# The table of token slots in a routed mixture-of-experts kernel: rows made list by list with scalars by partition, 64 places by 286 half blocks

## The chip, the cores and the metric

The kernel runs on one core of a Trainium2 chip, one launch. The metric is the device time of one execution in microseconds (us). The kernel before took 1169.23 us, the median of 3 runs (1165.0 to 1175.48).

Engines are named as in the profile: PE is TensorE (PEld its weight loads), DVE is VectorE, ACT is ScalarE, POOL is GpSimd, SP is SyncE. Every engine works through its own instructions in order.

## The reference

The kernel computes one layer on 8 sequences of 512 tokens with 512 features:

```
xn = layernorm(x)
s  = attention(xn)      # 16 heads of 32, chunks of 128, a decayed linear attention, gate, group norm, @ Wo
g  = silu(moe(xn))      # 16 experts, each token to its best 4, plus a shared expert
x  = x + s * g
```

and the part that matters here:

```
router_probs = softmax(flat @ gate_w.T)
routing_weights, selected_experts = top_k(router_probs, 4)
routing_weights = routing_weights / routing_weights.sum(-1)
mixed = sum over e of comb[:, e] * (silu(flat @ Wg[e]) * (flat @ Wu[e]) @ Wd[e])
```

There are 4096 tokens with 4 choices each: 16,384 pairs of a token and an expert.

## The kernel before

The work goes in four stages.

1. All sequences are normed, transposed and routed, and the shared expert is computed. Sequence 0 of the attention runs along.
2. The pairs are sorted by expert into blocks of 128 rows. `sort()` (lines 372 to 466) finds for each pair its position in the sorted order; an expert's rows begin at a multiple of 128, so there are at most `NB` = 143 blocks. `table()` (lines 469 to 559) turns this around: `slot[p, b]` is to be the token that stands in row p of block b. Sequence 1 of the attention runs along (`sequence(1, ...)`, line 1043).
3. Each block gathers its tokens' rows by `slot` (L1071, an indirect DMA on POOL), is multiplied with its expert's weights (L1112, L1133) and written back.
4. The other six sequences of the attention run, and each token gathers its four expert rows and adds them up.

The table is made from 128 lists (`TOPK * NT` = 4 choices by 32 tiles of tokens). A list holds one pair per partition, with its place in its block (`sp[:, 0]`, 0 to 127) and its block (`sp[:, 1]`, 0 to 142). For each list there are two matrices in f16 with a row per partition: `place` has the token's number at the pair's place and zeros elsewhere, `block` has a one at the pair's block. `place.T @ block` puts the tokens where they belong, and the sum over all lists is the table.

`make()` (L510, L513, L516) makes these rows on DVE, 8 lists in one instruction, by comparing a count with the positions, which are broadcast along the rows. For that the lists stand interleaved by four (`QUAD`): the elements of one list's row are four elements apart. L513 multiplies in the token's number for half the lists; ACT does it for the other half (`number()`, L524, one instruction per list, with a scalar by partition). PE multiplies list after list into one bank (L545, 128 matmuls of 143 columns), 16 lists in a group (`GROUP`); after each group DVE adds the bank to `acc` (L553, L555). L558 turns `acc` into `slot`. The scratch lies in the place of the last four experts' weights (`wexp`), so the profile calls these tiles `wexp`; the weights are loaded there when the table is done with each half (L537 on SP's queue, L1049 on ACT's).

What sets the order: `table()` is a generator. The attention's `value()` and `product()` call `between[0]()` after each of their matmuls on 128 contraction rows (lines 590 and 634), and each call runs the generator to its next `yield`. `sequence(1, ...)` makes 32 such calls; line 1044 runs what is left. `on_pe()` pins PE to the order in which the code is written; on the other engines a scheduler places the instructions when the program is built. The lines that the working uses beside these: L643 to L647 rotate a head group's queries and keys, L708 and L710 make its states, L720 masks its scores, L714 scales its queries, L742 and L746 make its output, L764 is a reciprocal in the group norm, L773 and L778 apply it, L785 projects. L236 and L1007 are two earlier instructions on DVE (the norm of x; a scaling of `wo`).

Of the kernel before, what the change touches and what calls it, by code (L numbers as in the profile page):

```python
# [10 lines left out]
F32 = mybir.dt.float32  # L11
# [4 lines left out]
AF = mybir.ActivationFunctionType  # L16
ALU = mybir.AluOpType
AX = mybir.AxisListType

P = 128  # L20
B, N, D = 8, 512, 512
# [4 lines left out]
NT = B * NC  # L26
KC = D // P
E, F, TOPK = 16, 128, 4
# [7 lines left out]
NB = (B * N * TOPK + E * (P - 1)) // P  # L36
WE = KC * 2 * F + D
# [3 lines left out]


SURE = B * N * TOPK // P + E // 2
QUAD = 4
LATE = 4
GROUP = 16


SWAP = [(i + HD // 2) % HD for i in range(HD)]
# [46 lines left out]
def tile_block(ctx: ExitStack, tc: tile.TileContext, a: dict, out: bass.AP):  # L96
    nc = tc.nc
# [7 lines left out]
    def bank(tag, name):  # L105
        return pp.tile([P, 512], F32, tag=tag, name=name, bufs={"a": 4, "k": 1, "m": 1, "d": 2}[tag])
# [11 lines left out]
    def load(pool, name, shape, dt=F32):  # L118
        t = pool.tile(shape, dt, tag=name, name=name, bufs=1)
        flat = t if len(shape) == 2 else t.rearrange(  # L120
            "p a b -> p (a b)" if len(shape) == 3 else "p a b c -> p (a b c)")
        nc.sync.dma_start(flat, a[name])
        return t
# [30 lines left out]
    ident = load(const, "ident", [P, P])  # L154
# [7 lines left out]
    token = load(const, "token", [P, NT])  # L162
# [27 lines left out]
    posi = p1.tile([P, TOPK, NT], I32, tag="posi", name="posi")  # L190

    sp = const.tile([P, 2, TOPK * NT], F16, tag="slot", name="sp")
# [11 lines left out]
    @contextmanager  # L204
    def on_pe():

        with tc.issue_after(last_pe[-1]) if last_pe else nullcontext():
            yield
        traced = nc.cur_bb.bb.instructions
        last_pe.append(next(  # L210
            i for i in reversed(traced) if i.engine == mybir.EngineType.PE))

    def behind(engine):

        last = next(
            (i for i in reversed(nc.cur_bb.bb.instructions) if i.engine == engine), None)
        return tc.issue_after(last) if last else nullcontext()
# [154 lines left out]
    def sort():  # L372
# [22 lines left out]
        at = p1.tile([P, E, NT], F32, tag="at", name="at")  # L395
# [40 lines left out]
        bl = p1.tile([P, 2, TOPK, NT], I32, tag="bl", name="bl")  # L436
        for r in range(TOPK):
            nc.gpsimd.tensor_tensor(oa[:, r], oh[:, r], at, ALU.mult)
            with behind(DVE):
                nc.vector.tensor_reduce(  # L440
                    pos[:, r], oa[:, r].rearrange("p e t -> p t e"), axis=AX.X, op=ALU.add)
            with behind(DVE):
                nc.vector.tensor_copy(posi[:, r], pos[:, r])
            with behind(DVE):
                nc.vector.tensor_scalar(bl[:, 0, r], posi[:, r], P - 1, None, ALU.bitwise_and)
            with behind(DVE):
                nc.vector.tensor_scalar(bl[:, 1, r], posi[:, r], 7, None, ALU.logical_shift_right)
            with behind(DVE):
                nc.vector.tensor_copy(
                    sp.rearrange("p w (r t) -> p w r t", t=NT)[:, :, r], bl[:, :, r])  # L450
            yield
# [17 lines left out]
    def table(room):  # L469

        half = room.bitcast(F16)
        free = [0]
        quads = GROUP // QUAD


        def part(*shape):
            n = int(np.prod(shape))
            free[0] += n  # L480
            flat = half[:, free[0] - n : free[0]]
            return flat.rearrange("p (q j) -> p q j", j=QUAD) if len(shape) == 2 else (
                flat.rearrange("p (u q j) -> p u q j", u=quads, j=QUAD))

        homes = [(part(quads, P, QUAD), part(quads, NB, QUAD))]
        free[0] = WE * LATE
        homes.append((part(quads, P, QUAD), part(quads, NB, QUAD)))
        count = part(NB, QUAD)
        half_token = half[:, free[0] : free[0] + NT]
        free[0] += NT  # L490
        nc.scalar.copy(half_token, token)
        acc = room[:, free[0] // 2 :][:, :NB]
        nc.gpsimd.iota(
            count, [[1, NB], [0, QUAD]], base=0, channel_multiplier=0,
            allow_small_or_imprecise_dtypes=True)

        def rows(of, n):
            return of.rearrange("p (u j) -> p u j", j=QUAD).unsqueeze(2).to_broadcast(
                [P, of.shape[-1] // QUAD, n, QUAD])

        def make(i):
            place, block = homes[i // GROUP % 2]
            for u in range(0, quads, 2):
                us = slice(u, u + 2)
                lists = slice(i + u * QUAD, i + (u + 2) * QUAD)

                def counts(n):
                    return count[:, :n].unsqueeze(1).to_broadcast([P, 2, n, QUAD])

                nc.vector.tensor_tensor(  # L510
                    place[:, us], counts(P), rows(sp[:, 0, lists], P), ALU.is_equal)
                if u == 0:
                    nc.vector.tensor_tensor(  # L513
                        place[:, us], place[:, us], rows(half_token[:, lists.start % NT :][
                            :, : 2 * QUAD], P), ALU.mult)
                nc.vector.tensor_tensor(  # L516
                    block[:, us], counts(NB), rows(sp[:, 1, lists], NB), ALU.is_equal)

        def number(i, some):
            place = homes[i // GROUP % 2][0]  # L520
            for j in range(max(some[0], GROUP // 2), some[1]):
                row = place[:, j // QUAD, :, j % QUAD]
                t = (i + j) % NT
                nc.scalar.activation(row, row, AF.Copy, scale=token[:, t : t + 1])  # L524

        yield
        make(0)
        for j in range(0, GROUP, QUAD):
            number(0, (j, j + QUAD))
            yield  # L530
        for i in range(0, TOPK * NT, GROUP):
            more = i + GROUP < TOPK * NT
            if more:
                make(i + GROUP)
            else:
                for e in range(E - LATE, E - LATE // 2):
                    nc.sync.dma_start(wexp[:, e, :], a["experts"][:, e, :])  # L537
            if i < TOPK * NT // 2:
                yield
            place, block = homes[i // GROUP % 2]  # L540
            pn = bank("a", f"pn_{i}")
            for some in ((0, 5), (5, 10), (10, GROUP)):
                with on_pe():
                    for j in range(*some):
                        nc.tensor.matmul(  # L545
                            pn[:, :NB], lhsT=place[:, j // QUAD, :, j % QUAD],
                            rhs=block[:, j // QUAD, :, j % QUAD], start=(j == 0),
                            stop=(j == GROUP - 1))
                if more:
                    number(i + GROUP, some)  # L550
                if some[1] == GROUP:
                    if i:
                        nc.vector.tensor_tensor(acc, acc, pn[:, :NB], ALU.add)  # L553
                    else:
                        nc.vector.tensor_copy(acc, pn[:, :NB])  # L555
                yield
        t = const.tile([P, NB], I32, tag="slot", name="slot")
        nc.vector.tensor_scalar(t, acc, float(B * N // 2), None, ALU.add)  # L558
        slots.append(t)


# [17 lines left out]
    kept, carry, blocked = [], [], []  # L579
# [391 lines left out]
    def first():  # L971
# [22 lines left out]
        next(sorting)  # L994

    sorting = sort()
    norm(0)
    turn(0)
# [33 lines left out]
    wexp = exps.tile([P, EA - 1, WE], F32, tag="wexp", name="wexp")  # L1032
# [5 lines left out]
    for i in range(SURE, NB):  # L1038
        nc.sync.dma_start(y_d[i * P : (i + 1) * P, :], none)
    filling = table(wflat[:, (E - LATE) * WE :])  # L1040
    next(filling)
    between[0] = lambda: next(filling, None)
# [16 lines left out]
    more = att.tile([P, 2 * NC * D], U16, tag="v", name="more", bufs=2)  # L1059
    homes = [blkp.tile([P, ROW], U16, tag=f"xg{j}", name=f"xg{j}") for j in range(4)]  # L1060
# [136 lines left out]
    place = comb.tile([P, TOPK, NT], I32, tag="place", name="place")  # L1197
# [166 lines left out]
```

## Time and profile before

| what | us |
|---|---|
| median of 3 runs | 1169.23 |
| the profiled execution's own time | 1169.4 |
| its span, first to last instruction | 1167.6 |
| PE busy in the span | 1134.0 (97%) |
| DVE, ACT, POOL busy | 705.6, 460.2, 452.2 |
| first instruction of the table on DVE (L510) | at 227.61 |
| `slot` written (L558) | at 301.66 |
| first gather by it (L1071) | at 302.81 |
| first expert matmul (L1112) | at 318.61 |
| mean granted clock of TensorE | 0.996 |

A line of a group reads: line, engine, operation, output<-inputs, output shape<-input shape, count; then the busy time and the mean length of one in ns; then the idle time of the engine before these instructions and what ended it. A line of the order in time reads: start, time until the last end, engine, line, operation, tiles, shapes, count, and in brackets an idle time before it. An instruction's length runs into the next one's: on DVE the next starts some 0.08 us before the end of the one before. So the price of an instruction in a row of its kind is the time from start to start. A line of busy times by stretch gives the stretch, its length, then for PE, PEld, DVE, ACT and POOL the busy us (and the instructions), the granted clock, the busy share of the DMA engines and their GB/s.

### The profile page before, as it was taken

The page shows a single profiled execution, that of the slowest core. Times are in us where ns is not written, and L with a number is a line of the kernel's source. Part 1 is how long each engine was busy: PE and PEld are TensorE (multiplying, and loading weights), DVE is VectorE, ACT ScalarE, POOL GpSimd, SP SyncE. Part 2 cuts the span into 40 slices and gives each one's busy share as a digit, 9 for nine tenths or more (in the row PEclk, how much of TensorE's full clock was granted, in tenths as well). Part 3 has the DMA queues.
Part 4 walks back from the last instruction along what each step waited for, and adds up shares of the span by engine and source line. Part 5 has one row for each costly group of instructions (what it writes and reads, how often), then busy time and mean ns, then how long its engine had stood idle before and what let it go on. Part 6 is the DMA issues. An engine that isn't in the chain of part 4 may idle for free. (4 is left out here: it accounts for less than half of the span.)

```text
span 1167.6 us, 21692 instructions
## 1 busy us (share of the span) xinstructions
PE 1134.0 (97%) x7780; PEld 694.6 (59%) x7780; DVE 705.6 (60%) x1496; ACT 460.2 (39%) x1042; POOL 452.2 (39%) x432
## 2 busy tenths in 40 slices
PE   7999999989999999999999999999999999999997
PEld 3445554455577677777777775555554645545553
DVE  6358735996134344444444443968879598697784
ACT  3323324254364444444444442352252532523541
POOL 3213103200223333333333331782886858858211
PEclk9999999998999999999999999999999999999999
DMA  9975521290769989999999996951846637535012
GB/s 341 330 251 186 179 106 46 101 361 2 232 153 227 219 228 219 229 233 218 230 223 231 230 226 159 359 148 64 277 128 181 215 100 255 154 119 153 28 38 72
DMA packets 163787, 217.45 MB, mean 186 GB/s; under 512 B 89824, under 2 KB 99168, under 8 KB 161760
## 3 DMA queue, kind: packets, MB, share of 16 engines
q1 hardware_dynamic: 142272, 144.14, 41.9%
q0 software_dynamic: 21120, 70.34, 22.3%
q8 instruction: 65, 1.06, 0.4%
q10 hardware_dynamic: 288, 1.57, 0.4%
q14 instruction: 42, 0.34, 0.1%
HBM read 125.73 MB, written 72.43 MB: 170 GB/s over the span
## 5 line engine op out<-in xcount | busy, mean ns | idle before, releaser
L1112 PE MATMUL pgu<-wexp,xt 128*128 x1088 | 257.9, 380 | 2.7 <-ACT xt L1093 2.2
L1112 PEld LDWEIGHTS pgu<-wexp,xt 128*128 128x128 f32 x1088 | 205.8, 190 | 90.4 <-issue 29.5
L1071 POOL DMA_INDIRECT xg<-xn_d,slot x79 | 74.9, 948 | 243.0 <-DVE y L1142 156.4
L1095 ACT COPY xt<-pl 128x512 uint16<-128x512 uint16 x136 | 104.3, 767 | 142.9 <-DMA pl<-xg 75.9
L1117 DVE TENSOR_TENSOR slb<-slb,pgu 128x128 f32<-128x128 f32 x136 | 39.1, 288 | 196.6 <-ACT slb L1116 196.5
L1215 POOL DMA_INDIRECT yg<-y_d,place x128 | 142.4, 1112 | 31.4 <-issue 18.4
L1133 PE MATMUL py<-wexp,hT 128*128 x272 | 139.2, 594 | 0.0
L587 PE MATMUL pv<-wv,xT 128*128 128x512 f32 x256 | 122.2, 614 | 3.8 <-DMA xT<-xT_d 2.8
L631 PE MATMUL pk<-xT,wk 128*128 128x512 f32 x256 | 118.3, 603 | 0.0
L631 PE MATMUL pq<-xT,wq 128*128 128x512 f32 x256 | 115.9, 593 | 0.3 <-PEq L1177 0.3
L785 PE MATMUL pw<-wo,on 128*128 128x512 f32 x224 | 100.6, 596 | 5.5 <-DVE m L1253 4.9
L1071 POOL DMA_INDIRECT more<-xn_d,slot x57 | 53.8, 944 | 108.3 <-DVE y L1142 107.4
L1257 POOL TENSOR_TENSOR xo<-xo,m 128x512 f32<-128x512 f32 x31 | 45.3, 1461 | 128.4 <-DVE m L1253 121.2
L720 DVE TENSOR_TENSOR sc<-ps,dmask 128x512 f32<-128x512 f32 x128 | 79.1, 677 | 0.9 <-PE ps L695 0.8
L631 PEld LDWEIGHTS pq<-xT,wq 128*128 128x128 f32 x256 | 47.2, 191 | 52.8 <-issue 51.3
L587 PEld LDWEIGHTS pv<-wv,xT 128*128 128x128 f32 x256 | 46.6, 195 | 50.3 <-issue 42.8
L631 PEld LDWEIGHTS pk<-xT,wk 128*128 128x128 f32 x256 | 46.2, 190 | 50.0 <-issue 47.6
L1142 DVE TENSOR_SCALAR y<-py,xg 128x512 f32<-128x512 f32 x79 | 59.2, 750 | 27.4 <-PE py L1133 27.2
L785 PEld LDWEIGHTS pw<-wo,on 128*128 128x128 f32 x224 | 41.2, 190 | 54.9 <-issue 45.4
L1116 ACT ACTIVATE slb<-pgu 128x128 f32<-128x128 f32 x136 | 37.8, 278 | 80.0 <-PE pgu L1112 79.7
L704 ACT COPY blocked<-state 32x96 f32<-32x96 f32 x96 | 30.6, 319 | 79.0 <-DVE state L699 78.1
L1142 DVE TENSOR_SCALAR y<-py,more 128x512 f32<-128x512 f32 x57 | 42.7, 750 | 20.0 <-PE py L1133 20.0
(173 smaller groups left out, 1729.9 us busy)
## 6 DMA issues: line engine op xcount, KB each, us to landing
y_d<-y SPq DMA_DIRECT2D x136, 256.0 KB, 2.9
wexp<-in_experts SPq DMA_DIRECT2D x14, 768.0 KB, 7.8
sh_d<-sh SPq DMA_DIRECT2D x32, 256.0 KB, 3.1
m<-sh_d SPq DMA_DIRECT2D x32, 256.0 KB, 4.4
xo<-in_x SPq DMA_DIRECT2D x32, 256.0 KB, 3.8
out<-xo SPq DMA_DIRECT2D x31, 256.0 KB, 2.0
x<-in_x SPq DMA_DIRECT2D x7, 1024.0 KB, 7.6
xT_d<-xT SPq DMA_DIRECT2D x7, 1024.0 KB, 6.5
```

The lines of the kernel that those rows point to most:

```text
L587: nc.tensor.matmul(pv, lhsT=xT_of[b][:, k, t * P : (t + 1) * P], rhs=wv[:, k, :], start=(k == 0), stop=(k == KC - 1))
L631: nc.tensor.matmul(ps, lhsT=w[:, k, g * P : (g + 1) * P], rhs=xT_of[b][:, k, :], start=(k == 0), stop=(k == KC - 1))
L720: nc.vector.tensor_tensor(s, pss[j].rearrange("p (c t) -> p c t", t=C), dmask[:, g * HG + j].unsqueeze(1).to_broadcast([P, NC, C]), ALU.mult)
L785: nc.tensor.matmul(pw, lhsT=on_of[b][:, g, t * P : (t + 1) * P], rhs=wo[:, g, :], start=(g == 0), stop=(g == G - 1))
L1071: nc.gpsimd.indirect_dma_start(out=row(i), out_offset=None, in_=xn_d, in_offset=bass.IndirectOffsetOnAxis(ap=slot[:, i : i + 1], axis=0))
L1095: nc.scalar.copy(xt[:, KP:, :].bitcast(U16).rearrange("p k (t h) -> p h k t", h=2), turned(i).rearrange("p (h k) t -> p h k t", h=2))
L1112: nc.tensor.matmul(pg[:, : 2 * F], lhsT=xt[:, k, :], rhs=wflat[:, bass.ds(off + k * 2 * F, 2 * F)], start=(k == 0), stop=(k == KC - 1))
L1117: nc.vector.tensor_tensor(sl, sl, pg[:, F : 2 * F], ALU.mult)
L1133: nc.tensor.matmul(py, lhsT=hT_of.pop(i), rhs=wflat[:, bass.ds(off_of.pop(i) + KC * 2 * F, D)], start=True, stop=True)
L1142: gone.append(nc.vector.tensor_scalar(y, py, row(i).bitcast(F32)[:, bass.ds(at, 1)], None, ALU.mult).ins)
L1215: nc.gpsimd.indirect_dma_start(out=yg, out_offset=None, in_=y_d, in_offset=bass.IndirectOffsetOnAxis(ap=place[:, r, g : g + 1], axis=0))
L1257: nc.gpsimd.tensor_tensor(xo, xo, m, ALU.add)
```

## The change

The table is split otherwise. A position is cut into 64 places (`HALF`) and half blocks, 286 of them. A list's two rows, 64 and 286 elements, stand side by side without gaps, and each is made by one DVE tensor_scalar of its own, whose operands are scalars by partition: the list's place and the token's number for the first, the list's half block for the second. So DVE issues two instructions per list, 256 in all, and ACT's scalings go. PE multiplies lists in pairs: even ones into the upper 64 partitions of the bank, odd ones into the lower 64, each with 286 columns. After a group, now of 12 lists, DVE adds the bank, 286 columns, to `acc`, which is f16. At the end two matmuls with a folded identity (`fold`) add the two halves of the partitions and bring the half blocks to their places. `sp` is copied to f32 (`at`), as scalars are read from there. Each call of the generator makes four or five lists and, where a group is complete, issues that group's matmuls.

```diff
-QUAD = 4
 LATE = 4
-GROUP = 16
+GROUP = 12
+HALF = P // 2
...
-                nc.vector.tensor_scalar(bl[:, 0, r], posi[:, r], P - 1, None, ALU.bitwise_and)
+                nc.vector.tensor_scalar(bl[:, 0, r], posi[:, r], HALF - 1, None, ALU.bitwise_and)
...
-                nc.vector.tensor_scalar(bl[:, 1, r], posi[:, r], 7, None, ALU.logical_shift_right)
+                nc.vector.tensor_scalar(bl[:, 1, r], posi[:, r], 6, None, ALU.logical_shift_right)
...
         half = room.bitcast(F16)
+        lists, width = TOPK * NT, HALF + 2 * NB
+        early = half[:, : GROUP * width]
+        kept = half[:, WE * LATE :]
+        homes = [of[:, : GROUP * width].rearrange("p (j w) -> p j w", w=width)
+                 for of in (kept, early)]
...
-        nc.scalar.copy(half_token, token)
-        acc = room[:, free[0] // 2 :][:, :NB]
+        at = part(2 * 2 * lists).bitcast(F32)
+        count, acc, fold = part(2 * NB), part(2 * NB), part(HALF)
+        nc.vector.tensor_copy(at, sp.rearrange("p w l -> p (w l)"))
+        for h in range(0, P, HALF):
+            nc.scalar.copy(fold[h : h + HALF], ident[h : h + HALF, h : h + HALF])
         nc.gpsimd.iota(
-            count, [[1, NB], [0, QUAD]], base=0, channel_multiplier=0,
+            count, [[1, 2 * NB]], base=0, channel_multiplier=0,
             allow_small_or_imprecise_dtypes=True)
...
+        def rows(i):
+            home = homes[i // GROUP % 2][:, i % GROUP]
+            nc.vector.tensor_scalar(
+                home[:, :HALF], count[:, :HALF], at[:, i : i + 1],
+                token[:, i % NT : i % NT + 1], ALU.is_equal, ALU.mult)
+            nc.vector.tensor_scalar(
+                home[:, HALF:], count, at[:, lists + i : lists + i + 1], None, ALU.is_equal)
+
+        def add(g, n):
+            pn = bank("a", f"pn_{g}")
+            with on_pe():
+                for j in range(n):
+                    h = j % 2 * HALF
+                    home = homes[g % 2][:, j]
+                    nc.tensor.matmul(
+                        pn[h : h + HALF, : 2 * NB], lhsT=home[:, :HALF], rhs=home[:, HALF:],
+                        start=(j < 2), stop=(j >= n - 2))
+            if g:
+                nc.vector.tensor_tensor(acc, acc, pn[:, : 2 * NB], ALU.add)
+            else:
+                nc.vector.tensor_copy(acc, pn[:, : 2 * NB])
 
         yield
...
+        made = added = calls = 0
+        while added * GROUP < lists:
+            if made >= min(lists, (added + 1) * GROUP):
+                add(added, min(GROUP, lists - added * GROUP))
+                added += 1
+                if (added + 1) * GROUP >= lists > added * GROUP:
+                    for e in range(E - LATE, E - LATE // 2):
+                        nc.sync.dma_start(wexp[:, e, :], a["experts"][:, e, :])
+            for _ in range(4 + calls % 2):
+                if made < min(lists, (added + 2) * GROUP):
+                    rows(made)
+                    made += 1
+            calls += 1
             yield
...
+        pt = bank("a", "pslot")
+        with on_pe():
+            for h in range(2):
+                nc.tensor.matmul(
+                    pt[h * HALF : (h + 1) * HALF, :NB], lhsT=fold,
+                    rhs=acc.rearrange("p (b h) -> p b h", h=2)[:, :, h], start=True, stop=True)
         t = const.tile([P, NB], I32, tag="slot", name="slot")
-        nc.vector.tensor_scalar(t, acc, float(B * N // 2), None, ALU.add)
+        nc.vector.tensor_scalar(t, pt[:, :NB], float(B * N // 2), None, ALU.add)
         slots.append(t)
```

The functions `make()`, `number()`, `counts()` and the old `rows()`, and the loop that called them, go.

## The prediction before the run

> **What bounds the kernel now.** I read the page first, then the busy time by stretch, then the order in time of DVE and PE in the stretch where the table is made, then the groups by shape.
>
> The page: engine, busy time, instructions.
> ```profile
> PE 1134.0 (97%) x7780; PEld 694.6 (59%) x7780; DVE 705.6 (60%) x1496; ACT 460.2 (39%) x1042; POOL 452.2 (39%) x432
> ```
> PE sets the time nearly everywhere, so a microsecond that PE loses early is not given back. The table is made between 227 and 303 us. Busy time there, first of all instructions, then of those that touch `wexp` alone (the table's scratch lies in it):
> ```profile
> 227.00:303.00 76.00, 70.09 (x781) 43.97 (x779) 55.10 (x106) 38.08 (x98) 1.24 (x3) 0.96 0.52 193
> 227.00:303.00 76.00, 20.68 (x128) 14.91 (x128) 28.60 (x49) 22.18 (x64) 0.58 (x1) 0.96 0.52 193
> ```
> The columns are PE, PEld, DVE, ACT, POOL, granted clock. PE is idle for 5.9 us of 76; DVE for 20.9. So PE bounds this stretch, and DVE can take some 20 us more before it does. DVE's order, where the prices of its instructions stand (start, length until its last end, xcount):
> ```profile
> 227.61 0.69 DVE L510 TENSOR_TENSOR wexp<-wexp,sp 128x1024 f16<-128x1024 f16 x1 [1.66 <-POOL wexp L493]
> 228.22 0.75 DVE L516 TENSOR_TENSOR wexp<-wexp,sp 128x1144 f16<-128x1144 f16 x1
> 228.88 0.68 DVE L513 TENSOR_TENSOR wexp<-wexp 128x1024 f16<-128x1024 f16 x1
> ...
> 34.41 1.67 DVE L1007 TENSOR_SCALAR wo<-wo,nw 128x512 f32<-128x512 f32 x4 [4.86 <-DMA wo<-in_wo]
> ...
> 26.23 1.91 DVE L236 TENSOR_SCALAR x<-x,mv,rstd 128x512 f32<-128x512 f32 x4 [1.00 <-POOL rstd L250]
> ...
> 225.68 0.18 DVE L463 TENSOR_SCALAR eoff<-ef 128x36 int32<-128x36 f32 x1
> 225.77 0.18 DVE L465 TENSOR_SCALAR eoff<-ef 128x36 int32<-128x36 f32 x1
> ...
> 251.90 0.30 DVE L553 TENSOR_TENSOR wexp<-wexp,pn 128x143 f32<-128x143 f32 x1
> 252.12 0.69 DVE L510 TENSOR_TENSOR wexp<-wexp,sp 128x1024 f16<-128x1024 f16 x1
> ...
> 301.32 0.30 DVE L553 TENSOR_TENSOR wexp<-wexp,pn 128x143 f32<-128x143 f32 x1 [3.35 <-PE pn L545]
> 301.66 0.23 DVE L558 TENSOR_SCALAR slot<-wexp 128x143 int32<-128x143 f32 x1
> 302.67 2.48 DVE L778 TENSOR_TENSOR on<-on,pb 128x512 f32<-128x512 f32 x4 [0.77 <-PE pb L773]
> ```
> What counts is the time from one start to the next. An f16 tensor_tensor of 1024 takes 0.61 (227.61 to 228.22), one of 1144 0.66: 120 elements in some 0.063, so 1.92 per ns, and about 0.067 us fixed. PE in the same stretch:
> ```profile
> 236.79 0.82 PE L545 MATMUL pn<-wexp 128*128 128x143 f16 x5
> 237.43 1.04 PE L631 MATMUL pq<-xT,wq 128*128 128x512 f32 x2
> ...
> 243.74 1.08 PE L742 MATMUL po<-sc,v 128*32 128x128 f32 x32
> ...
> 263.58 3.54 PE L587 MATMUL pv<-wv,xT 128*128 128x512 f32 x4 [2.77 <-DMA xT<-xT_d]
> ```
> Five lists hold PE for 0.64, so 0.13 a list and some 16.5 for 128. L742, four column groups side by side, starts 32 matmuls in 0.9, or 0.028 each.
>
> **The change, part by part.**
>
> *PE.* 128 matmuls of 143 columns at 0.13 become 128 of 286 columns on half the array. Bounds from both sides: 0.028 (L742) and twice the columns with no overlap, 0.26. Pairs on two column groups, as in L742, and rows without gaps make about 0.07 to 0.13 likely: a gain of 0 to 8 us, if PE still set the pace. The fold adds two matmuls and a wait: 0.5 us.
>
> *ACT.* 64 scalings (22.2 us) go, two copies come. ACT waited 20 us for DVE at these; nothing on PE waited long for them (1.1). Worth 0 to 1; I take 0.
>
> *POOL and queues.* The iota halves (1.32, on the way to the first row): −0.3, which the new cast of `sp` to f32 on DVE takes back. The loads of the last four experts move with the table's end; before, they were issued at 296.7 and 301.4, took some 7, and the first block read them at 318.6. They keep that distance. The gathers wait for `pb` as well as for the table and move with both. 0.
>
> *DVE, the step that decides.* Away go 16 L510, 16 L516, 8 L513: 16 × (0.60 + 0.66) + 8 × 0.60 = 25.0. In come 256 tensor_scalars with scalars by partition. What such a scalar costs is shown in f32: four L1007 (one scalar) last 1.67, their own length is 0.48, so (1.67 − 0.48)/3 = 0.396 from start to start; four L236 (two scalars) (1.91 − 0.54)/3 = 0.457. At two elements per cycle (0.267 for 512; faster than the 0.533 of L778, so two it is) 0.129 and 0.190 are left. Less the 0.067 that any instruction pays, a scalar costs 0.062, and the second one as much again. The immediate form L463 (0.09 for 36) pays none. L1142 agrees from PSUM: its mean is 750 ns against 679 of L778, the same size without a scalar.
>
> The rate of an f16 tensor_scalar is in no row. Its bounds are one element per cycle (L778) and four: L1007 gets double L778's rate by its form, L510 gets double by f16, and both apply to the new rows. I take four, by these two rows, the nearest, and keep two and one for the rivals.
> - place, 64 elements, two scalars: 0.067 + 0.124 + 0.017 = 0.208
> - block, 286 elements, one scalar: 0.067 + 0.062 + 0.074 = 0.203
>
> A list costs 0.41, and 128 cost 52. Eleven adds of 286 from PSUM, at 0.22 for L553's 143 (251.90 to 252.12) plus 0.15, make 4.1. The other DVE work of the stretch: 16 L720 at 0.60, 4 rotations of 2.42 (L643, L645, L646, L647), 3 L714 at 0.46, 4 L746 at 0.60, 4 states at 0.42, a reciprocal of 0.87, the slot 0.21: 25.8. Sum 82. The first row can start at about 227.3, so DVE alone is not through before 309.3, where it now starts L778 at 302.67.
>
> [...]
>
> *What DVE waits for.* Walking the built order of the two engines side by side, DVE mostly has rows to go on with while PE waits for rows (the longest such wait of PE, for lists 36 to 47, is about 9 us, because a score product, a rotation and the state of the next head group stand between). DVE itself waits at the end: `on` of the last group (about 306.4) goes through ACT's squares, PE's `pr`, a table load and the square root before the reciprocal. That chain takes 4.5 now (292.07 to 296.53); only two lists stand in it: 1.9 lost. Then the last add, the fold (0.6), and `pb`, which PE starts after the last piece of `pv` and the fold (1.8). L778 then starts at about 313.7, 11.0 later. To this come waits between dependent instructions, hidden now in part by rows (0.5), and PE at a lowered clock after its waits (0.87 to 0.96 was granted around its 2.8 us wait for xT; the profile's stretches around 260 to 290): 1. So some 12.5 later. PE's gain of 0 to 8 is lost in PE's waits for DVE.
>
> After L778 PE is the bound again, and the shift passes to the end in full. The profiled execution took 1169.4 (span 1167.6), the median of the runs is 1169.23; they agree. 1169.4 + 12.5 = 1182.
>
> **The rivals.**
> 1. *Two elements per cycle in f16 too.* For it: no row shows the two doublings together. A list then costs 0.017 + 0.074 = 0.091 more, 128 cost 11.7: 1194. At one per cycle it is 0.276 × 128 = 35 more: 1217; against it, L1007 is already at two.
> 2. *The scalars are free in short instructions, and PE stays the bound* (the other side). A list then costs 0.067 + 0.017 + 0.067 + 0.074 = 0.225, 29 in all, and DVE needs 59 of 75. PE, whose lists fall from 0.13 to 0.07, gains up to 8, of which the wait for xT (2.8) and the end chain leave 5 to 6: 1164. It decides when a list costs DVE less than about 0.30: the 75.4 from 227.3 to 302.67, less 25.8, 4.1 and the end waits of some 5, leave 40 for 128. Against it: all 8 instructions of L1007 and L236 above pay, and the short L710 (one scalar) has 245 ns where the copy L708 of the same 32 elements has 182.
> 3. *The two lists do not run side by side*, so the change does not do what it says on PE. At 0.26 a list PE needs 70 + 16.5 = 86.5 for the stretch, as much as DVE, and the two add waits to each other: some 5 more, 1187. For it: L742's groups have 32 columns and f32. Against it: they do overlap there.
>
> **How the numbers follow.** Chances: forecast 0.63, with a range of its own of 1175 to 1189 (5 ns a scalar or an instruction more or less is some 2 to 3 us, the end chain 3, the clock 2); two per cycle 0.18; one per cycle 0.04; free scalars 0.07; not side by side 0.08. The predicted time is the forecast's, 1182. A range from 1174 to 1196 holds about 0.60 + 0.13 + 0.08 = 0.81. About 1% (11.7 us) is what a measurement of this kernel can tell from no change. Slower by more than that begins at 1180.9: 0.36 of the forecast's 0.63, and rivals 1 and 3, 0.66. Within 1%: 0.27 of the forecast and 0.05 of the free scalars, 0.32. Faster 0.02.
>
> **What would show it.** Right: DVE without a gap from 227 to about 307; the place rows and block rows both near 0.20 from start to start (each some 85 ns longer in duration), though one has 64 elements and the other 286; PE idle waiting for `wexp` rows of DVE for 10 to 20 us, the longest before the fourth add; the slot near 311 and L778's successor near 314; after it the order in time as before, shifted. Block rows of 0.28 show rival 1. Wrong: rows of about 0.11 on average, PE without waits and lists at 0.07 (rival 2); or PE matmuls of the table that take more than 0.2 a list (rival 3). If DVE is idle by more than 10 us in the stretch, my walk of its waits fails.

## The result and the profile after

The changed kernel took 1186.27 us, the median of 4 runs (1183.3 to 1187.98), beside 1172.36 for the kernel before, now the median of 4 (1165.0 to 1176.64). The ratio is 1.0114, with a 95% interval of 1.0082 to 1.0146. The prediction was 1182.0, with a range of 1174 to 1196. The profiled execution took 1183.3 (span 1181.5, mean clock 0.992), 13.9 more than that of before. Lines are 20 lower than before in most of the file: L778 is now L758, L720 is L700, L553 is L512, L545 is L508, L1112 is L1092.

The page, as before engine, busy time, share, instructions:
```profile
PE 1138.8 (96%) x7782; PEld 690.8 (58%) x7782; DVE 736.0 (62%) x1716; ACT 440.6 (37%) x979; POOL 450.2 (38%) x432
```
DVE has 30.4 us more than before; PE has 4.8 more, though its work for the table shrank. The same stretch as before, of all instructions, and then a longer one that reaches to the end of the table, of all instructions and of those that touch `wexp`:
```profile
227.00:303.00 76.00, 59.98 (x605) 31.86 (x604) 74.78 (x293) 12.48 (x26) 0.52 (x1) 0.91 0.43 170
...
227.00:317.00 90.00, 72.09 (x782) 38.14 (x780) 83.87 (x327) 17.07 (x34) 1.79 (x3) 0.92 0.45 171
...
227.00:317.00 90.00, 16.19 (x130) 8.72 (x130) 58.73 (x268) 0.00 (x0) 0.00 (x0) 0.92 0.45 171
```
The bound has changed sides. Before, PE was busy for 70.1 of these 76 us and DVE for 55.1; now DVE is busy for 74.8 and PE for 60.0. The stage needs 90 us, and PE is idle for 17.9 of them. DVE's order in time, first the first row of the table, then among the rows, then at the end of the stage:
```profile
227.25 0.54 DVE L496 TENSOR_SCALAR wexp<-wexp,token 128x64 f16<-128x64 f16 x1
```
```profile
228.19 0.29 DVE L496 TENSOR_SCALAR wexp<-wexp,token 128x64 f16<-128x64 f16 x1
228.40 0.28 DVE L499 TENSOR_SCALAR wexp<-wexp 128x286 f16<-128x286 f16 x1
228.60 0.29 DVE L496 TENSOR_SCALAR wexp<-wexp,token 128x64 f16<-128x64 f16 x1
...
305.82 0.45 DVE L512 TENSOR_TENSOR wexp<-wexp,pn 128x286 f16<-128x286 f16 x1
306.19 0.29 DVE L496 TENSOR_SCALAR wexp<-wexp,token 128x64 f16<-128x64 f16 x1
...
308.25 0.67 DVE L726 TENSOR_TENSOR on<-po,on 128x512 f32<-128x512 f32 x1
...
311.66 0.95 DVE L744 RECIPROCAL rs<-rs 128x128 f32<-128x128 f32 x1 [1.91 <-ACT rs L740]
313.02 0.45 DVE L512 TENSOR_TENSOR wexp<-wexp,pn 128x286 f16<-128x286 f16 x1 [0.40 <-PE pn L508]
314.23 0.31 DVE L538 TENSOR_SCALAR slot<-pslot 128x143 int32<-128x143 f32 x1 [0.77 <-PE pslot L534]
316.37 2.48 DVE L758 TENSOR_TENSOR on<-on,pb 128x512 f32<-128x512 f32 x4 [1.83 <-PE pb L753]
```
A place row (64 elements, two scalars by partition) and a block row (286, one scalar) both take 0.205 from start to start, so a list takes 0.41. An add takes 0.37 (305.82 to 306.19). L758 starts at 316.37 where L778 started at 302.67: 13.7 later, nearly all of the 13.9. Counted from DVE's first row (227.61 before, 227.25 now) the stage grew from 75.05 to 89.11, by 14.1. PE's order in the same stretch:
```profile
237.35 0.92 PE L508 MATMUL pn<-wexp 128*64 128x286 f16 x12 [4.09 <-DVE sc L700]
...
242.90 0.92 PE L508 MATMUL pn<-wexp 128*64 128x286 f16 x12
243.75 1.13 PE L611 MATMUL pq<-xT,wq 128*128 128x512 f32 x2
...
255.43 1.64 PE L508 MATMUL pn<-wexp 128*64 128x286 f16 x12 [4.23 <-DVE sc L700]
...
260.56 0.92 PE L508 MATMUL pn<-wexp 128*64 128x286 f16 x12
```
Twelve lists hold PE for 0.85 (242.90 to 243.75), 0.07 a list with the gaps around them; the single instructions start in pairs, 0.12 from one pair to the next. So two lists do run side by side. What PE does with the time won is in its waits (total, times, longest):
```profile
PE pn L508 <- DVE sc L700: 11.1, 4, 4.2
PE pn L508 <- DVE wexp L499: 1.7, 1, 1.7
```
The weight loads wait 8.2 more for place rows. All three wait for DVE.

Behind the stage the shift passes on. The first expert matmul starts 15.2 later than before (333.77), the load of `place` with which the last stage begins 13.0 later (740.65 against 727.62), and the end is 13.9 later. That stage and end agree to a few tenths is luck: from the start of L758 or its counterpart to the end, the profiles of the runs below take 861.9 to 869.0, but for three on a slower chip; before and changed happen to take 864.9 and 865.1.

### The profile page after: what moved, and what is told of

Same layout as the page of the kernel before. It is cut to its first block, busy times and chain, and to the rows that moved or that the text cites. A ratio compares the mean times of both kernels' runs of the same rounds, so it can differ in the third digit from the quotient of the medians.

```text
span 1181.5 us, 21839 instructions
## 1 busy us (share of the span) xinstructions
PE 1138.8 (96%) x7782; PEld 690.8 (58%) x7782; DVE 736.0 (62%) x1716; ACT 440.6 (37%) x979; POOL 450.2 (38%) x432
## 5 line engine op out<-in xcount | busy, mean ns | idle before, releaser
L1092 PE MATMUL pgu<-wexp,xt 128*128 x1088 | 257.8, 380 | 3.0 <-ACT xt L1073 2.7
L1092 PEld LDWEIGHTS pgu<-wexp,xt 128*128 128x128 f32 x1088 | 206.2, 190 | 90.3 <-issue 29.9
L611 PE MATMUL pk<-xT,wk 128*128 128x512 f32 x256 | 120.7, 614 | 0.0
L611 PEld LDWEIGHTS pq<-xT,wq 128*128 128x128 f32 x256 | 48.1, 194 | 55.1 <-issue 53.4
L700 DVE TENSOR_TENSOR sc<-ps,dmask 128x512 f32<-128x512 f32 x128 | 79.1, 677 | 0.9 <-PE ps L675 0.9
```

What stands on the lines that cost most here:

```text
L611: nc.tensor.matmul(ps, lhsT=w[:, k, g * P : (g + 1) * P], rhs=xT_of[b][:, k, :], start=(k == 0), stop=(k == KC - 1))
L700: nc.vector.tensor_tensor(s, pss[j].rearrange("p (c t) -> p c t", t=C), dmask[:, g * HG + j].unsqueeze(1).to_broadcast([P, NC, C]), ALU.mult)
L1092: nc.tensor.matmul(pg[:, : 2 * F], lhsT=xt[:, k, :], rhs=wflat[:, bass.ds(off + k * 2 * F, 2 * F)], start=(k == 0), stop=(k == KC - 1))
```

## The experiments

The theory: DVE decides the stage, and its rows cost 0.067 fixed, 0.062 for each scalar by partition, and their elements at four a cycle. One a cycle stands for L778's rate in the profile before, an estimate from its four instructions: 0.60 from start to start less the 0.067, so 512 elements in 0.533 or 0.96 per ns. The first rival was that a row costs 0.205 whatever it holds, which the equal lengths of the two rows suggest as well. The second was that PE decides the stage.

| kernel | median us | ratio to before, 95% | L758's successor starts | from DVE's first row to it |
|---|---|---|---|---|
| before | | 1 | 302.67 | 75.05 |
| changed | 1186.27 | 1.0114 (1.0082 to 1.0146) | 316.37 | 89.11 |
| second scalar | 1190.43 | 1.0173 (1.0144 to 1.0201) | 324.06 | 95.17 |
| second immediate | 1183.49 | 1.0118 (1.0087 to 1.0150) | 315.57 | 89.31 |
| count in f32 | 1194.69 | 1.0209 (1.0173 to 1.0245) | 327.54 | 98.66 |
| places together | 1170.26 | 0.9989 (0.9967 to 1.0010) | 300.93 | 73.73 |
| not in turn | 1186.33 | 1.0132 (1.0106 to 1.0157) | 316.93 | 89.92 |
| control | 1184.36 | 1.0118 (1.0094 to 1.0141) | 316.79 | 89.14 |
| immediates | 1164.01 | 0.9949 (0.9929 to 0.9969) | 296.57 | 69.71 |
| places together, other bank | 1167.38 | 0.9973 (0.9952 to 0.9993) | 300.19 | 72.52 |
| sums twice | 1194.17 | 1.0101 (1.0056 to 1.0146) | 318.21 | 90.94 |
| other bank | 1196.24 | 1.0111 (1.0064 to 1.0157) | 315.97 | 88.44 |
| places on POOL | 1200.93 | 1.0122 (1.0075 to 1.0169) | 320.73 | 90.75 |
| shared rows | 1168.02 | 0.9982 (0.9964 to 0.9999) | 300.08 | 72.33 |

The kernel before took 1170.3 to 1172.4 beside these, except beside "sums twice", "other bank" and "places on POOL", which ran on another chip where it took 1184.38. Read those three by their ratios. The first row of the table starts anywhere from 226.3 to 230.0 in these profiles, so the lengths in the last column are to be compared, not the starts in the one before it.

**A second scalar, and a second immediate, in the block row.** Only the second operand differs between these two.

```diff
-                home[:, HALF:], count, at[:, lists + i : lists + i + 1], None, ALU.is_equal)
+                home[:, HALF:], count, at[:, lists + i : lists + i + 1], one, ALU.is_equal,
+                ALU.mult)
```
(`one` is a 128 x 1 tile of ones; the other kernel has `1.0` in its place.)

> The block row gets a second scalar by partition, a tile of ones that it multiplies by; what is computed stays. The theory of the prediction: VectorE decides the stage, and a row costs 0.067 fixed, 0.062 for each scalar by partition, and its elements at four a cycle. The block row then goes from 0.205 start to start to 0.267 and the list from 0.411 to 0.47; 128 x 0.062 = 7.9 us more, the median from 1186.3 to about 1194 (1192 to 1197). The rival, that a row of these widths costs 0.205 whatever it holds (place and block rows took the same in the trace, 64 elements with two scalars and 286 with one): 0.205 still, 1186. A second rival, that TensorE decides the stage: the row grows by 0.062 but the time by less than 3 us.

> The block row gets a second operation, a multiplication by the constant 1.0 that is part of the instruction. The theory (the scalar by partition costs, not the second operation): the row stays at 0.205 and the time at 1186.3 (within 2 us). The rival, that a second operation costs as much as its scalar: 0.267 and 1194, as in the run with a tile of ones.

DVE's order with the scalar, the first row and then among the rows; the block row is L501 here:
```profile
228.89 0.70 DVE L498 TENSOR_SCALAR wexp<-wexp,token 128x64 f16<-128x64 f16 x1
```
```profile
229.78 0.35 DVE L501 TENSOR_SCALAR wexp<-wexp,one 128x286 f16<-128x286 f16 x1
230.04 0.29 DVE L498 TENSOR_SCALAR wexp<-wexp,token 128x64 f16<-128x64 f16 x1
230.25 0.35 DVE L501 TENSOR_SCALAR wexp<-wexp,one 128x286 f16<-128x286 f16 x1
```
The block row takes 0.26 and the list 0.47 (229.78 to 230.25). The stage ends 7.7 later than in the changed kernel, but it also began 1.6 later (228.89 against 227.25): it is 6.1 longer, and 5.9 longer than with the immediate. The execution is 6.9 longer than with the immediate, and the immediate costs nothing (there both rows stay at 0.205). 7.9 was expected, and the median lies below the 1192 to 1197 that were given; that with the immediate is 2.8 below 1186.3, where 2 was allowed. The kernel before, too, took 2.1 less beside these two than beside the changed one. The rest of the 7.9 filled waits that DVE had anyway: its 1.1 before one add is gone, and its wait for the square root is 1.48 instead of 1.91. So the scalar is paid for, not the second operation, and what does not fill a wait of DVE reaches the stage's end. A fixed price of 0.205 and a PE that decides are both out.

**The count in f32.** `count` gets twice the bytes: `part(4 * NB).bitcast(F32)` for `part(2 * NB)`.

> The counting row that both rows are compared with is held in f32 instead of f16; what is computed stays. The theory, four elements a cycle in f16 and two with an f32 operand: 286 elements take 0.149 instead of 0.074 and 64 take 0.033 instead of 0.017, so the block row goes from 0.205 to 0.28, the place row to 0.22, the list from 0.411 to 0.50; 128 x 0.091 = 11.7 us more, 1198 (1196 to 1201). The rival, that the rows do not go at four a cycle in f16 and the scalars cost less than 0.062: no change, 1186.

DVE's order, among the rows:
```profile
229.64 0.36 DVE L499 TENSOR_SCALAR wexp<-wexp 128x286 f16<-128x286 f32 x1
229.92 0.30 DVE L496 TENSOR_SCALAR wexp<-wexp,token 128x64 f16<-128x64 f32 x1
230.14 0.36 DVE L499 TENSOR_SCALAR wexp<-wexp 128x286 f16<-128x286 f32 x1
```
The list takes 0.50 and the block row 0.28, as expected. The stage is 9.5 longer than in the changed kernel (its end is 11.2 later, its first row 1.6), and the time is 11.2 above that with the immediate, though the median is again below the range given (1196 to 1201). Of the 11.7 expected, 1.1 and 0.5 filled the same two waits of DVE. Less 0.129 for the fixed part and the scalar, the 286 elements take 0.15 here and, from the 0.205 of the changed kernel, 0.076 in f16. The f16 row therefore goes at twice this rate, 3.8 per ns, which is the four a cycle that the prediction took. This was its least certain price.

**No scalars at all.** The rows get constants (`float(i % HALF)`, `float(i)`), so the table leaves out where the tokens belong, and a control with the same plain slots goes beside it. The edit of the control:

```diff
-        nc.vector.tensor_scalar(t, pt[:, :NB], float(B * N // 2), None, ALU.add)
+        for c in range(0, NB, NT):
+            w = min(NT, NB - c)
+            nc.vector.scalar_tensor_tensor(
+                t[:, c : c + w], pt[:, c : c + w], 0.0, token[:, :w], ALU.mult, ALU.add)
+        nc.vector.tensor_scalar(t, t, float(B * N // 2), None, ALU.add)
```

> The control for the next run. The table is made as before, but the slot numbers are not taken from it: each gets a number from the row of token numbers (the sum is multiplied by zero), so that the blocks gather other rows than the reference asks for. Ten short VectorE instructions come behind the last sum, some 1.5 us by the 0.18 of a row of 16 elements. Both theories: the stage ends 1 to 2 us later than in the changed kernel and the rest is as it was: 1186 to 1189.

> As the control before, and every scalar by partition of the rows becomes a constant in the instruction, so the rows hold other numbers (the table is wrong, and the slots do not depend on it). The theory: without the scalars a place row costs 0.067 + 0.017 = 0.084 and a block row 0.067 + 0.074 = 0.141, the list 0.225 instead of 0.411, 23.8 us less of VectorE's work; TensorE then decides the stage as where the places were made together (69 of VectorE's 78 us busy, TensorE waiting for its bank): 15 to 19 us less than the control. The rival, a row costs 0.205 whatever its scalars: as the control.

The control took 1184.36, below the 1186 to 1189 given, and its stage is as long as the changed kernel's (89.14): its added instructions shorten DVE's wait for `pb` behind them, from 1.83 to 1.30. DVE's order without scalars:
```profile
228.13 0.17 DVE L496 TENSOR_SCALAR wexp<-wexp 128x64 f16<-128x64 f16 x1
228.21 0.23 DVE L498 TENSOR_SCALAR wexp<-wexp 128x286 f16<-128x286 f16 x1
228.36 0.17 DVE L496 TENSOR_SCALAR wexp<-wexp 128x64 f16<-128x64 f16 x1
```
The place row takes 0.08, the block row 0.15, the list 0.23 (expected 0.225). Two scalars were 0.125 and one 0.055 to 0.06. The time falls by 20.4 against the control, 1 to 5 more than expected, to below that of the kernel before; the stage is 19.4 shorter. So the 256 rows as such were affordable; their 384 scalars were not. This is also where rival 2 of the prediction would have ended: it gave 1164, and the median is 1164.01. That they agree so closely is chance, as the kernel before stood at 1170.77 beside this run and not at 1169.4.

**TensorE, less side by side.** `h = (j >= n // 2) * HALF` instead of `j % 2 * HALF`, with the starts and stops of the two halves.

> The lists of a group go to the two halves of TensorE's output one half after the other (the first six lists to the upper 64 places, then the last six to the lower) instead of in turn, so no two lists stand side by side; rows, sums and all of VectorE stay, and so does what is computed. The theory: VectorE decides the stage, so TensorE may take 0.12 or more for a list instead of 0.061 (12 lists in 1.5 us instead of 0.75) and the time stays at 1186 (0 to 2 more, from the two or three places where VectorE waits for a sum). The rival, that TensorE decides the stage: 128 x 0.061 = 7.8 us more, 1194.

PE's order, one group with its rows ready:
```profile
243.57 1.19 PE L508 MATMUL pn<-wexp 128*64 128x286 f16 x12
```
The time stayed and the stage is 0.8 longer, but the test is weak: a group takes 1.19 instead of 0.92. Six lists of one half alone take 0.92 in the same run (at 265.05), so in the twelve some of the two halves still overlapped. The edit gave PE at most 0.27 for each of 10.7 groups, 2.9, not the 7.8 that the rival reckons with. Hence the next one.

**The sums twice.**

```diff
-                for j in range(n):
-                    h = j % 2 * HALF
+                for i in range(2 * n):
+                    j, h = i // 4 * 2 + i % 2, i % 2 * HALF
...
-                        start=(j < 2), stop=(j >= n - 2))
+                        start=(i < 2), stop=(i >= 2 * n - 2))
```

> Each pair of lists goes through TensorE twice into the same sum, and the folding matrix holds 0.5 instead of 1, so what is computed stays; VectorE's work is the same. A pair takes 0.121 at full clock, so 64 more pairs are 7.7 us more of TensorE, and more where its clock is halved. The theory (VectorE decides the stage, TensorE's added time comes out of its waits, 18 of 90 us): 0 to 2 us more than the changed kernel, 1184 to 1188, the little from the places where VectorE waits for a sum. The rival, TensorE decides the stage: 8 us more, 1192 to 1195.

PE's order, the same group:
```profile
243.52 1.65 PE L509 MATMUL pn<-wexp 128*64 128x286 f16 x24
```
0.73 more for a group is 7.8 for all. The stage is 1.8 longer (90.94), the ratio is 1.0101 where 8 us more would be 1.018 or above, outside its interval. PE's added work comes out of its waits.

**Another bank.** `bank("d", ...)` instead of `bank("a", ...)` for the sums (a bank is the buffer in which PE builds a sum).

> The changed kernel with the sum of twelve lists in a bank of the pool of the products and outputs instead of the pool that the scores fill. The theory: the 11.1 us in which TensorE's sums wait for the scores' banks cost nothing while VectorE decides: 0 to 2 us less, 1183 to 1187. The rival: these waits are what the stage lost: 5 to 11 us less, 1175 to 1181.

PE's waits:
```profile
PE pn L508 <- DVE wexp L499: 4.2, 3, 2.1
PE pn L508 <- DVE wexp L514: 3.9, 1, 3.9
```
The waits for the scores' banks are gone, others for DVE stand in their place, and the stage is 0.7 shorter (ratio 1.0111): DVE's wait of 1.1 before one add is gone. The longest waits of PE were slack but for that. The stage shows this; the interval of the ratio would still hold the 5 us at the rival's lower end (1.007).

**The places of twelve lists together.** Two f16 tensor_tensor of 768 replace twelve place rows; the block rows stay. The core of the edit:

```diff
+            place, block = homes[i // GROUP % 2]
+            if i % GROUP == 0:
+                n = min(GROUP, lists - i)
+                q = n // QUAD
+                nc.vector.tensor_tensor(
+                    place[:, :q], apart.rearrange("p (n j) -> p n j", j=QUAD).unsqueeze(
+                        1).to_broadcast([P, q, HALF, QUAD]), each(sp[:, 0, i : i + n]), ALU.is_equal)
+                nc.vector.tensor_tensor(
+                    place[:, :q], place[:, :q], each(number[:, i : i + n]), ALU.mult)
...
-                        pn[h : h + HALF, : 2 * NB], lhsT=home[:, :HALF], rhs=home[:, HALF:],
+                        pn[h : h + HALF, : 2 * NB], lhsT=place[:, j // QUAD, :, j % QUAD],
+                        rhs=block[:, j],
```

> The place rows of twelve lists are made together, without scalars: two tensor_tensor in f16, places interleaved by four, one comparing with the place numbers and one multiplying by the token numbers; the block rows stay as they are, and TensorE still takes two lists side by side. Theory: 768 elements at two a cycle and a fixed part are about 0.47 each, 0.94 for twelve lists or 0.078 each, so the list takes VectorE 0.205 + 0.078 = 0.283 instead of 0.411, 16 us less in 128 lists; the stage comes near to what TensorE needs (72 us of its 90 now), so 13 to 18 us less: 1168 to 1173. The rival, that the weights of TensorE, now four elements apart, slow it to the 0.131 a list of the kernel before: TensorE is the bound by some 8 us, 1174 to 1180.

DVE's and then PE's order in this kernel:
```profile
227.19 0.55 DVE L512 TENSOR_TENSOR wexp<-wexp,sp 128x768 f16<-128x768 f16 x1
227.66 0.29 DVE L517 TENSOR_SCALAR wexp<-wexp 128x286 f16<-128x286 f16 x1
227.87 0.55 DVE L515 TENSOR_TENSOR wexp<-wexp 128x768 f16<-128x768 f16 x1
228.34 2.34 DVE L517 TENSOR_SCALAR wexp<-wexp 128x286 f16<-128x286 f16 x11
230.59 0.55 DVE L512 TENSOR_TENSOR wexp<-wexp,sp 128x768 f16<-128x768 f16 x1
```
```profile
239.19 0.95 PE L526 MATMUL pn<-wexp 128*64 128x286 f16 x12
```
Twelve lists take DVE 3.4 (227.19 to 230.59), 0.283 each. The stage is 15.4 shorter than the changed kernel's, and the time is that of the kernel before (0.9989). Weights four elements apart cost PE 0.03 in twelve lists, so that rival is out.

**That kernel with the other bank, and with a sixth of its block rows on POOL.**

> The kernel with the places of twelve lists made together, and the sum of twelve lists goes to a bank of another pool of PSUM (the one of the products and outputs) instead of the pool that the scores fill; what is computed stays. The theory: VectorE is no longer the bound there (it waits 3.1 us for the square root at the end), TensorE is, and the 7.5 us in which its sums wait for VectorE to empty the scores' banks lie on the path: 3 to 7 us less than the 1170.3 of that kernel, 1163 to 1167. The rival, that VectorE still decides between the waits, so that the wait only moves: 1169 to 1171. A second rival, that the products now wait for the sums' bank: 1171 to 1174.

> The kernel with the places made together and its sums in the other pool of banks, and every sixth block row (22 of 128) is made on GpSimd instead of VectorE; what is computed stays. In that kernel VectorE still has no gap of over 0.4 us from 227 to 292. If VectorE still sets the stage there, 22 x 0.205 = 4.5 us leave its path and the time falls by 2 to 4, until TensorE is the bound (66 of 76 us busy): ratio to the kernel before 0.9973 becomes about 0.994 to 0.996. The rival, TensorE sets the stage by now: the time of that kernel, 0.997. A second rival, GpSimd's rows (0.65 for 64 elements; some 0.8 to 2 for 286) come too late in their group: slower than it, 1.000 or more.

With the other bank the stage is 1.2 shorter where 3 to 7 were expected, and 1.0 of it is a wait of DVE for a sum that is gone. The median is 2.9 lower, but the two kernels ran on different chips and their ratios (0.9989 and 0.9973) have intervals that overlap, so what the bank alone brings stays open. What fell is the reason given: most of PE's 7.5 us of waits were not on the path there either. DVE's order at the end of its rows:
```profile
291.22 0.70 DVE L517 TENSOR_SCALAR wexp<-wexp 128x286 f16<-128x286 f16 x3
291.83 0.68 DVE L745 TENSOR_TENSOR on<-po,on 128x512 f32<-128x512 f32 x1
295.46 0.95 DVE L763 RECIPROCAL rs<-rs 128x128 f32<-128x128 f32 x1 [2.95 <-ACT rs L759]
```
From its first row (227.67) to L745 DVE stands idle for 0.04 us, and only then waits for the square root: up to there it still sets the stage. So 22 of its rows went to POOL, and that did not help either (a stage of 72.33, ratio 0.9982): the groups of the block rows on the two engines show why.
```profile
L517 POOL TENSOR_SCALAR wexp<-wexp 128x286 f16<-128x286 f16 x22 | 27.2, 1248 | 31.0 <-PE pn L526 30.8 <-DVE wexp L490 0.3
L517 DVE TENSOR_SCALAR wexp<-wexp 128x286 f16<-128x286 f16 x106 | 26.9, 317 | 0.0
```
DVE's rows last 317 ns in the mean instead of 288. Sorted by what runs beside them, 57 with no POOL row beside them last 283 in the mean, and the 49 that overlap one 358, up to 579. From start to start DVE's 106 rows take 25.0 us where its 128 took 26.3, so 3.3 of the 4.5 us that were taken off it are lost again. Its other instructions take 0.7 longer, and its way from the first row to L745 falls by 0.5 only (64.2 to 63.7). So the run leaves open what a DVE with less to do would bring there.

**All places on POOL.** `nc.gpsimd` for the place row of the changed kernel, with the sums in the other bank.

> The place rows are made on GpSimd instead of VectorE by the same instruction, and the sums go to the other pool of banks; what is computed stays. The theory: VectorE's list falls from 0.411 to 0.205, 26 us less in 128 lists, and the stage goes to what TensorE needs, 1160 to 1167, if GpSimd takes up to 0.55 for a row (its 572 numbers of counting took 1.32, 0.15 for 64; its 128x4 row with tensor_scalar 0.27). The rival, GpSimd takes over 0.6 a row or slows VectorE's rows while it runs: GpSimd or VectorE is the bound and little is won, 1175 to 1190.

The rows on POOL, and DVE's longest wait:
```profile
L496 POOL TENSOR_SCALAR wexp<-wexp,token 128x64 f16<-128x64 f16 x128 | 83.3, 673 | 0.9 <-DVE wexp L487 0.9
```
```profile
DVE wexp L512 <- PE pn L508: 21.4, 9, 4.7
```
The rival holds: 128 rows at 0.65 are 83 us, so POOL is the bound of a stage of 90.75, and DVE, with half its rows gone, waits 21 us for sums whose places are missing.

## Why the prediction was right, point by point

- *The bound and the mechanism: right.* From 227.25 to 309.7 DVE has one gap of note, of 1.1, and the stage follows DVE's rows but for what fills its waits (6.1 longer for 7.9 of rows, 9.5 for 11.7, and 19.4 shorter for 23.8 where DVE waits more for PE and the square root).
- *A list at 0.41, rows at 0.208 and 0.203: right.* Both measure 0.205. The fixed part, the 0.062 for a scalar and the four a cycle each have a run that confirms them (0.08 and 0.15 without scalars; 0.06 for one more; 0.28 for 286 in f32).
- *The end of the stage: right in its parts.* The waits at the reciprocal, the fold and `pb` are 1.91, 0.77 and 1.83, where 1.9, 0.6 and 1.8 were given; the wait at the last add, 0.40, had no entry.
- *What was too small.* L758 starts 13.7 later, not 12.5. The undersized term is the one for waits and the clock, put at 1.5 and measured at 2.7 (316.37 against 313.7): the last group's L726 already starts 1.85 later than reckoned (308.25 against 306.4). 1.1 of that is DVE's wait before one add (261.55): with 50 of its 128 place rows made, the add stood next in its order and PE was late with the sum. The median, 1186.27, is 4.3 above the number given: 1.4 because the change cost 13.9 and not 12.5, and 3.0 because the kernel before now stands at 1172.36 and the prediction added to 1169.4.
- *PE's waits: right in size, wrong in place.* Idle 17.9 us where 10 to 20 were given, and the gain of its faster lists was all lost in them. But the longest was to be some 9 us, for rows before the fourth sum. It is 4.2, before the third, and it is for a bank: the sums take theirs from the pool that four score products fill, and these are emptied by L700, which DVE has queued among the rows. The fourth sum starts at 260.56 without a wait. The run with the other bank shows that this error cost at most 0.7.
- *PE's list: just below the lower end,* 0.061 a list in pairs, where 0.07 to 0.13 was taken. Without effect while DVE decides, as the doubled sums show.
- *Queues and experts' loads at 0: nearly.* From L758 to the first expert matmul it takes 17.4 in this profile and took 15.9 before. The last copy of `so` on ACT waits for an earlier store:

```profile
332.86 0.59 ACT L948 COPY so<-pw 128x512 f32<-128x512 f32 x1 [4.56 <-DMA s_d<-so]
```
The late experts' loads of ACT's queue (313.01 and 315.29) and the first gathers share that time; that they delay the store is argued, not shown. In the run with the second immediate the distance is 16.0, in the one with the second scalar 15.7, so it is not a fixed price of the change. It is gone again by 740.65, which is 13.0 later than before.
- *The rivals.* Two elements a cycle and free scalars are both refuted by rows: the block row takes 0.205 and not 0.28, and the two rows take 0.205 in the mean and not 0.11. That the lists do not run side by side is refuted by the pairs of 0.12.

## What to carry to other kernels

Price a short VectorE instruction by its operands, not by its elements alone: here 64 elements with two scalars by partition cost as much as 286 with one, and the scalars were 24 of the 53 us of rows. Before an engine with slack is given many small instructions to relieve the bound, set its new sum against that slack: 82 against 75 made it the bound, and what the other engine won became waiting. To get the good half, keep the part that helps TensorE (286 columns without gaps, in pairs) and make the short rows in few long instructions: 0.9973 (0.9952 to 0.9993) of the time before, with the sums in another pool's bank.

## What the runs showed of the hardware beside this

- A tensor_scalar that took DVE 0.205 takes POOL 0.65 (64 elements, two scalars) or 0.99 to 1.85 (286, one scalar).
- DVE and POOL slow each other, though not always. Beside POOL's rows of 286, some of DVE's f16 block rows last 0.44 to 0.58 instead of 0.28, while the f32 masks of the scores (L719) keep their 0.68. Beside POOL's rows of 64, DVE's block rows keep 0.292; there POOL pays, with 0.85 for a row beside five block rows and 0.57 for one beside the masks (L700). The lengthening does not last as long as POOL's row, as far as POOL's spans can be trusted: in the kernel with shared rows, a DVE row that starts 0.11 into a POOL row is done 0.4 before the POOL row ends.

```profile
249.96 1.05 POOL L517 TENSOR_SCALAR wexp<-wexp 128x286 f16<-128x286 f16 x1
```
```profile
250.07 0.53 DVE L517 TENSOR_SCALAR wexp<-wexp 128x286 f16<-128x286 f16 x1
```
Why rows of one form are lengthened and the f32 masks are not, and why DVE is spared beside the rows of 64, stays open.
